# The shared expert's parts moved among the encoder's last two sequences, with VectorE norms in closer slots for these and a gate computed on GpSimd

## The chip, the cores and the metric

The kernel runs on one core of a Trainium2 chip. The metric is the device time of one execution in microseconds (us). Engines are named as in the profile: PE is TensorE, PEld its weight loads, DVE is VectorE, ACT is ScalarE, POOL is GpSimd, SP is SyncE, which issues most of the DMAs.

## The reference, cut to what matters

Eight sequences of 256 tokens with 128 features pass through four blocks with residual additions. The change touches the end of the first (six encoder layers) and the second (a mixture of experts); the third is a state-space block, the fourth two layers of local attention.

```python
x = x + encoder(layernorm(x))              # 6 layers, 16 heads
x = x + experts(layernorm(x))              # 8 experts, top 1, and a shared one
x = x + state_space(layernorm(x))
x = x + local_attention_layers(layernorm(x))

# one encoder layer
w_avg = softmax(q k^T / sqrt(8)).mean(over heads)
sa = softmax(w_avg + rel) @ h
h1 = LN(h + sa, l1);  h2 = LN(h1, l2)
ff = relu(h2 @ w1.T + b1) @ w2.T + b2
h  = LN(h2 + ff, l3)

# experts, per token
score = x @ router; e = argmax(score); gate = sigmoid(score[e])
routed = silu(gate*x @ w1[e]) * (gate*x @ w3[e]) @ w2[e]
shared = silu(x @ ws1) * (x @ ws3) @ ws2
out = routed + shared
```

Everything is fp32; F is 352 in the experts and 512 in the encoder.

## The kernel before, in words

**Order of work.** Within each of the stages the order of all instructions is written out by hand. `at(slot, order, fn)` puts a step into a table; the steps are then issued by slot, within a slot by `order`, and within that in order of insertion (routes first, then shared parts and blocks, then the encoder's plans). Each engine has a queue that takes its instructions in this order and waits at the first whose data aren't there. A slot is thus a place in the order and no time.

**Encoder.** `plan(n, l, b)` lays out layer l of sequence b, with n = 8l + b from 0 to 47 and t0 = 16n: the attention scores and their exponentials fill the slots t0-12 to t0+19, the rest of the layer follows in the `r_` steps, from the transpose of the mixing weights (t0+21) by mix (t0+29), norm 1 (t0+32), norm 2 (t0+36), transpose (t0+38), the feed-forward network (two halves `r_ff1` at t0+40 and t0+44, `r_ff2` at t0+47) to norm 3 (t0+58). So two to three sequences overlap. `r_norm1`, `r_norm2`, `r_residual` and `r_norm3` run on POOL, by the helpers `normal_pool` (L247, L249) and `affine` (L102, L103); mean and variance (`mean_var`, L235, L237) run on DVE, and 1/sqrt as an addition and a power on POOL (`rsqrt`, L81, L82). In the last layer norm 3 also adds the sequence into x (L481). The softmax weights need `dg` (L332) from POOL and the row sums' inverse `z` (L330) from DVE.

**Routing.** `route(b, t0)` follows each sequence of the last layer from its slot t0+59 on, one step a slot: statistics, 1/sqrt, norm (POOL), transpose (PE, L556), copy (ACT, L560), scores (PE, L565), `choose` (six DVE operations from L573 to L582; L577 is one of them; and exp(-top) on ACT, L584), `count` (PE, L594 to L598), `gate` (DVE, L588, L589: 1/(1 + exp(-top))), `put` (DVE: positions in the bucket, to L612), and `send` (POOL: scaling by the gate, L617, and two scatter DMAs, L619, into the bucket in HBM).

**Experts.** Behind the last route `table` (DVE, from L633 to L657) counts the blocks of each expert, and PE and SP load the results into registers. `shared(q, t0)` is the shared expert for sequences 2q and 2q+1: three times two matmuls (`up`, L750), Silu on ACT (L757), product on DVE (L761), `down` (PE, L767), copy (ACT, L771), transposes (PE, L776), two additions into x (DVE, L781). Parts 0 and 1 stand between table and blocks, parts 2 and 3 behind the blocks. `block(j, t0)` is one of 23 blocks of 128 routed tokens: load from the bucket (SP, L687), transpose (PE, L692), up, Silu, product, transpose, down, copy (DVE, L734) and store to `routed` (SP, L735).

**After the experts.** The state-space stage begins with a gather of `routed` (POOL, four indirect DMAs for two sequences, L887), the additions (DVE, L894), a norm, a transpose, a convolution (PE) and Silu (ACT, L978). Behind the experts SP issues the loads of the last stage's weights (L1148), whose tiles lie where the experts' weights were.

**PSUM.** `bank()` takes the next of six banks, which the attention scores use also; `small_bank()` one of two, which everything else of the encoder uses.

Of the kernel before, what the change touches and what calls it, by code (L numbers as in the profile page):

```python
# [10 lines left out]
F32 = mybir.dt.float32  # L11
# [7 lines left out]
P = 128  # L19
# [36 lines left out]
def model_kernel(ctx: ExitStack, tc: tile.TileContext, A: dict, out: bass.AP):  # L56
# [42 lines left out]
    def affine(dst, src, w, b):  # L99

        shape = [P, src.shape[1], P]
        nc.gpsimd.tensor_tensor(dst, src, w.unsqueeze(1).to_broadcast(shape), ALU.mult)  # L102
        nc.gpsimd.tensor_tensor(dst, dst, b.unsqueeze(1).to_broadcast(shape), ALU.add)  # L103
# [77 lines left out]
    with ExitStack() as s0:  # L181
# [63 lines left out]
        def normal_pool(dst, src, mv, rs):  # L245
            neg = small.tile([P, NC], F32, name="neg", tag="neg", bufs=2)
            nc.gpsimd.tensor_scalar(neg, mv[:, :, 0], -1.0, None, ALU.mult)  # L247
            for i in range(NC):
                nc.gpsimd.tensor_scalar(  # L249
                    dst[:, i, :], src[:, i, :], neg[:, i : i + 1], rs[:, i : i + 1], ALU.add, ALU.mult  # L250
                )

        def plan(n, l, b):
            t0 = SLOTS * n
            v = {}

# [155 lines left out]
            def r_norm1():  # L412
                ln = v["w"][2]
                normal_pool(v["t1"], v["t1"], v["mv1"], v["rs1"])
                affine(v["t1"], v["t1"], ln[:, 0, :], ln[:, 1, :])

            def r_norm2():
                n2 = wk.tile([P, NC, P], F32, name="n2", tag="n2")
                normal_pool(n2, v["t1"], v["mv2"], v["rs2"])
                v["n2"] = n2  # L420

            def r_residual():
# [3 lines left out]
                affine(v["h2"], v["n2"], ln[:, 2, :], ln[:, 3, :])  # L426
# [47 lines left out]
            def r_norm3():  # L474
                ln = v["w"][2]
                hn = hp.tile([P, NC, P], F32, name="h", tag=f"h{b}")
                normal_pool(hn, v["t2"], v["mv3"], v["rs3"])
                affine(hn, hn, ln[:, 4, :], ln[:, 5, :])
                hs[b] = hn
                if l == DEPTH0 - 1:  # L480
                    nc.gpsimd.tensor_tensor(xs[b], xs[b], hn, ALU.add)  # L481
# [6 lines left out]
            at(t0 + 29, 4, r_mix)  # L488
            at(t0 + 30, 5, r_add)
            at(t0 + 31, 5, lambda: put("rs1", lambda: inv_std(v["mv1"], 1)))  # L490
            at(t0 + 32, 6, r_norm1)
            at(t0 + 35, 5, lambda: put("mv2", lambda: mean_var(v["t1"], 2)))
            at(t0 + 36, 5, lambda: put("rs2", lambda: inv_std(v["mv2"], 2)))
            at(t0 + 36, 6, r_norm2)
            at(t0 + 37, 6, r_residual)
            at(t0 + 38, 4, r_transpose2)
            at(t0 + 39, 5, r_h2t)
            at(t0 + 40, 4, lambda: r_ff1(0))
            at(t0 + 41, 5, lambda: r_relu(0))
            at(t0 + 44, 4, lambda: r_ff1(1))  # L500
            at(t0 + 45, 5, lambda: r_relu(1))
            at(t0 + 47, 4, r_ff2)
            at(t0 + 48, 5, r_add3)
# [1122 lines left out]
```

## Time and profile before

| what | us |
|---|---|
| median of 3 runs | 2029.11 (2028.04 to 2031.71) |
| profiled execution, its own time | 2033.83 |
| its span, first to last instruction | 2032.1 |
| busy in the span: PE, DVE, ACT, POOL | 1715.8, 1430.8, 1283.9, 1116.2 |
| norm 3 with x of sequence 7 (the last) ends | 1091.8 |
| last route's positions, table | 1101.6, 1104.6 |
| shared parts 0 and 1 on PE | 1107.0 to 1126.6 |
| blocks, to the last copy | 1126.6 to 1181.2 |
| shared parts 2 and 3, to the last addition | 1181.2 to 1198.9 |
| first addition of gathered rows begins | 1207.1 |

The table's places in time are us from the span's start. The page of the profile gives busy times, then the span in 40 slices (each digit the busy share in tenths, PEclk the granted TensorE clock), DMA queues, and the costliest groups of instructions. An engine that is busy three quarters of the span may set the time in one stage and idle in the next, so the stages are read one by one.

### The profile page before, as it was taken

The numbers are of one execution on the slowest core, as the hardware profiler recorded it, in microseconds if no ns is written. First come the engines' busy times: TensorE is split into PE (matmuls) and PEld (weight loads), VectorE is DVE, ScalarE is ACT, GpSimd is POOL, SyncE is SP. The second block draws the span as 40 slices with busy tenths as digits, with TensorE's granted clock in tenths as the row PEclk, the third lists the DMA queues.
The fourth block names the chain that finished last, engine by engine and source line by source line (L and its number), as shares of the span: only waits on it lengthen the run. The fifth ranks groups of instructions, "written<-read, shape, count | busy, mean of one in ns | idle before, by whom it ended". The sixth has DMA issues, their size and how long they took to land. (4 is left out here: it accounts for less than half of the span.)

```text
span 2032.1 us, 38679 instructions
## 1 busy us (share of the span) xinstructions
PE 1715.8 (84%) x13390; PEld 1009.4 (50%) x13406; DVE 1430.8 (70%) x3308; ACT 1283.9 (63%) x4576; POOL 1116.2 (55%) x1663
## 2 busy tenths in 40 slices
PE   5899999999999999997864968687676898888987
PEld 2565656565656566555542733122222655555554
DVE  4787787787878787876632435988897677666664
ACT  4887888888888888886520324544522666666654
POOL 2576777777777777776773024767464333233221
PEclk9999999999999999999975989888877899999989
DMA  9200000000000000000000120000000000000000
GB/s 305 66 2 1 24 2 2 14 11 2 15 10 2 9 17 2 2 1 6 4 8 12 41 93 4 5 6 1 0 0 1 1 1 1 1 1 1 6 6 11
DMA packets 43218, 35.52 MB, mean 17 GB/s; under 512 B 3957, under 2 KB 39055, under 8 KB 43023
## 3 DMA queue, kind: packets, MB, share of 16 engines
q1 hardware_dynamic: 41423, 30.63, 4.9%
q8 instruction: 108, 1.77, 0.4%
q0 software_dynamic: 1024, 2.10, 0.3%
q14 instruction: 87, 0.71, 0.1%
q10 hardware_dynamic: 576, 0.31, 0.1%
HBM read 20.57 MB, written 12.45 MB: 16 GB/s over the span
## 5 line engine op out<-in xcount | busy, mean ns | idle before, releaser
L322 ACT ACTIVATE e<-s,nmax 128x256 f32<-128x256 f32 x1536 | 709.1, 492 | 81.7 <-DVE nmax L318 77.9
L318 DVE TENSOR_REDUCE nmax<-s 128x2 f32<-128x512 f32 x768 | 493.6, 670 | 151.8 <-PE s L308 151.8
L322 ACT ACTIVATION_READ_ACCUMULATOR e<-s,nmax 128x1 f32 x1536 | 343.8, 224 | 0.0
L308 PE MATMUL s<-kt,qm 32*128 32x256 f32 x3072 | 305.1, 422 | 17.1 <-ACT e L322 14.5
L359 PE MATMUL pacc<-e,dg 128*32 128x256 f32 x3072 | 257.2, 396 | 41.3 <-POOL dg L332 27.9
L308 PEld LDWEIGHTS s<-kt,qm 32*128 32x128 f32 x3072 | 184.2, 189 | 114.9 <-ACT e L322 64.8
L1076 POOL TENSOR_TENSOR hc<-h,bc 128x1024 f32<-128x1024 f32 x64 | 155.5, 2434 | 116.1 <-DVE h L1069 109.7
L1298 POOL TENSOR_TENSOR r<-r,r 128x512 f32<-128x512 f32 x64 | 81.1, 1271 | 231.3 <-DVE r L1279 195.1
L332 POOL TENSOR_TENSOR dg<-sel,z 128x256 f32<-128x256 f32 x192 | 118.5, 617 | 133.8 <-DVE z L330 114.7
L1058 ACT ACTIVATE da<-pd,na 128x510 f32<-128x510 f32 x128 | 80.8, 682 | 167.8 <-PE pd L1041 156.1
L359 PEld LDWEIGHTS pacc<-e,dg 128*32 128x32 f32 x3072 | 95.6, 110 | 164.8 <-POOL dg L332 60.4
L1069 DVE TENSOR_TENSOR_SCAN h<-da,pu 128x1024 f32<-128x1024 f32 x64 | 146.3, 2287 | 8.5 <-ACT da L1058 0.5
L81 POOL TENSOR_SCALAR rs<-mv 128x2 f32<-128x2 f32 (+1 forms) x192 | 44.1, 230 | 191.5 <-DVE mv L237 96.5
L82 POOL TENSOR_TENSOR rs<-rs,mhalf 128x2 f32<-128x2 f32 (+1 forms) x192 | 139.4, 726 | 15.7
L1041 PE MATMUL pu<-u,ssel 32*128 32x512 f32 x256 | 97.5, 768 | 49.9 <-DVE h L1069 40.0
L1355 ACT ACTIVATE el<-sl,nm,rn 128x128 f32<-128x128 f32 x256 | 114.0, 466 | 39.5 <-DVE nm L1346 39.3
L1255 PE MATMUL pq<-wqkv,y 128*128 128x512 f32 x224 | 121.4, 629 | 1.0 <-issue 1.0
L369 ACT ACTIVATE nw<-pacc 128x256 f32<-128x256 f32 x96 | 36.9, 384 | 116.8 <-PE pacc L355 115.9
L447 PE MATMUL pf<-h2t,wa 128*128 128x256 f32 x384 | 106.9, 402 | 2.4 <-DVE h2t L436 2.4
L463 PE MATMUL po<-wf,r 128*128 128x128 f32 x768 | 104.9, 294 | 0.0
L463 PEld LDWEIGHTS po<-wf,r 128*128 128x128 f32 x768 | 96.9, 205 | 13.6 <-DVE st L235 13.6
L1067 DVE TENSOR_TENSOR pu<-pu,bc 128x1024 f32<-128x1024 f32 x64 | 77.8, 1215 | 19.9 <-PE pd L1041 19.8
(271 smaller groups left out, 3507.7 us busy)
## 6 DMA issues: line engine op xcount, KB each, us to landing
bucket<-zrow SPq DMA_DIRECT2D x1, 8640.0 KB, 29.5
ln<-in_ln_dram SPq DMA_DIRECT2D x6, 448.0 KB, 3.7
wa<-in_wa_dram SPq DMA_DIRECT2D x6, 384.0 KB, 3.1
wf<-in_wf_dram SPq DMA_DIRECT2D x6, 256.0 KB, 6.3
wqkv<-in_wqkv_dram SPq DMA_DIRECT2D x1, 1536.0 KB
xb<-bucket SPq DMA_DIRECT2D x23, 64.0 KB, 1.8
routed<-ob SPq DMA_DIRECT2D x23, 64.0 KB, 1.5
w<-in_w1e_dram SPq DMA_DIRECT2D x1, 1408.0 KB, 32.0
```

The source lines that it names most:

```text
L82: nc.gpsimd.tensor_tensor(dst, dst, mhalf.to_broadcast(list(dst.shape)), ALU.pow)
L308: nc.tensor.matmul(ss[g][:, i, :], v["qm"][rows, 2 * k + i].rearrange("p j q -> p (j q)"), v["kt"][rows, :], start=True, stop=True,)
L318: nc.vector.tensor_reduce(v["nmax", k][:, g, :], v["s", k][g], AX.X, ALU.max, negate=True)
L322: nc.scalar.activation(v["e", k][:, g, i, :], v["s", k][g][:, i, :], AF.Exp, bias=v["nmax", k][:, g, i : i + 1], accum_out=v["z", k][:, g, ...
L332: nc.gpsimd.tensor_tensor(dg, sel32.unsqueeze(1).to_broadcast(sh), z.unsqueeze(2).to_broadcast(sh), ALU.mult)
L359: nc.tensor.matmul(acc, v["dg", k][:, 2 * g + i, :], v["e", k][:, g, i, :], start=(g == 0), stop=False,)
L447: nc.tensor.matmul(pf[:, i, :], v["w"][0][:, f0 : f0 + P], v["h2t"], start=True, stop=True)
L463: nc.tensor.matmul(po[:, c, :], v["r"][:, f, c * P : (c + 1) * P], v["w"][1][:, f, :], start=(f == 0), stop=(f == 3),)
L1069: nc.vector.tensor_tensor_scan(h.rearrange("p h t -> p (h t)"), da, pu.rearrange("p h t -> p (h t)"), 0.0, ALU.mult, ALU.add)
L1076: nc.gpsimd.tensor_tensor(hc, v["h", n], v["bc", 1].unsqueeze(1).to_broadcast([P, 2, T2]), ALU.mult)
L1255: nc.tensor.matmul(pq, yb[:, col : col + P], wqkv[:, l, i * INNER : (i + 1) * INNER], start=True, stop=True)
L1355: nc.scalar.activation(v["e", c][:, par, j, :], v["s", c][par][:, j, :], AF.Exp, scale=v["rn", c][:, 0, h : h + 1], bias=v["nm", c][:, par ...
```

## The change

- **Closer slots.** For n of 46 and 47 (`tail`) the steps behind the attention stand closer: mix at t0+23 (was 29), norm 1 at t0+26, transpose at t0+30 (38), the second half of the network four slots behind the first's base (was six), norm 3 at t0+40 (58). Norm 3 of sequence 5 in the last layer stands at t0+50. Each route of the last layer follows its norm 3 by a slot.
- **Engines.** Norms 1, 2 and 3 of these two with their affines (not the residual's) and the last addition into x run on DVE; so do the norm and the scaling of `send` in routes 6 and 7. The 1/sqrt and the scatters stay on POOL. Routes 4 to 7 take their PSUM from the six banks.
- **Gate.** exp(-top) leaves ACT: POOL multiplies by -1 and raises e to that power, in the slot of `choose`, behind it.
- **Shared expert.** Part 0 begins at slot 776 (t0 of the last sequence, 752, and 24), part 1 at 790, part 2 at 798; the table stands at 804, part 3 at 805, the blocks from 814. `up` comes last in its slot now (order 8, was 4), and the parts use six-bank PSUM throughout. Nothing but a load of ACT's exponential table stands behind the blocks.

```diff
-        def normal_pool(dst, src, mv, rs):
+        def normal(eng, dst, src, mv, rs):
+            if eng is nc.vector:
+                for i in range(NC):
+                    eng.tensor_scalar(
+                        dst[:, i, :], src[:, i, :], mv[:, i, 0:1], rs[:, i : i + 1], ALU.subtract, ALU.mult
+                    )
+                return
...
+        last3 = [58] * (NB - 3) + [50, 40, 40]
...
+            tail = n >= DEPTH0 * NB - 2
+            eng = nc.vector if tail else nc.gpsimd
...
-                normal_pool(v["t1"], v["t1"], v["mv1"], v["rs1"])
-                affine(v["t1"], v["t1"], ln[:, 0, :], ln[:, 1, :])
+                normal(eng, v["t1"], v["t1"], v["mv1"], v["rs1"])
+                affine(eng, v["t1"], v["t1"], ln[:, 0, :], ln[:, 1, :])
...
-            at(t0 + 29, 4, r_mix)
...
-            at(t0 + 58, 6, r_norm3)
+            t1, t2, t3 = (t0 + 23, t0 + 30, t0 + 40) if tail else (t0 + 29, t0 + 38, t0 + 58)
+            if l == DEPTH0 - 1:
+                t3 = t0 + last3[b]
+            at(t1, 4, r_mix)
...
+            t2 = t2 + (4 if tail else 6)
...
+            at(t3, 6, r_norm3)
...
+        euler = c0.tile([P, 1], F32, name="euler", tag="euler")
+        nc.vector.memset(euler, np.e)
...
+            eng = nc.vector if b >= NB - 2 else nc.gpsimd
+
+            route_bank = bank if b >= NB - 4 else small_bank
...
-                nc.scalar.activation(top, top, AF.Exp, scale=-1.0)
                 v["top"] = top
+
+            def decay():
+
+                nc.gpsimd.tensor_scalar(v["top"], v["top"], -1.0, None, ALU.mult)
+                nc.gpsimd.tensor_tensor(v["top"], euler.to_broadcast([P, NC]), v["top"], ALU.pow)
...
-                at(t0 + k, 4, lambda k=k: up(k))
+                at(t0 + k, 8, lambda k=k: up(k))
...
-        first_free = SLOTS * (DEPTH0 * NB - 1) + 59
+        def exp_table():
+            nc.scalar.preload_act_table_set("natural_log_exp_and_others")
+
         for b in range(NB):
-            route(b, SLOTS * ((DEPTH0 - 1) * NB + b) + 59)
-        e0 = first_free + 11
+            route(b, SLOTS * ((DEPTH0 - 1) * NB + b) + last3[b] + 1)
+        end = SLOTS * (DEPTH0 * NB - 1)
+
+        shared(0, end + 24)
+        shared(1, end + 38)
+        shared(2, end + 46)
+        e0 = end + last3[-1] + 12
         at(e0, 1, table)
-        shared(0, e0 + 1)
-        shared(1, e0 + 4)
-        e1 = e0 + 12
+        shared(3, e0 + 1)
+        e1 = e0 + 10
         for j in range(MB):
             block(j, e1 + j)
         at(e1 + 4, 9, where)
-        e2 = e1 + MB + 3
-        shared(2, e2)
-        shared(3, e2 + 3)
+        at(e1 + MB + 4, 9, exp_table)
```

## The prediction

> **What bounds the kernel now.** I read the slices of the page first, to find the stages, then the chain, then stretches of 10 us, then each engine's queue in order of time. Columns of a queue row: start and length in us, engine, line, operation, out<-in; in brackets the idle time before it and what ended it.
>
> ```profile
> span 2032.1 us, 38679 instructions
> ...
> PE   5899999999999999997864968687676898888987
> ...
> POOL 2576777777777777776773024767464333233221
> PEclk9999999999999999999975989888877899999989
> ```
>
> A slice is 50.8 us. Slices 20 to 23 (1016 to 1219 us) hold the end of the encoder, the routing, the experts and the gather; PE drops and its clock falls to half. The chain of waits does not reach so far back (its longest pieces begin at 1569 us), so here the queues must speak.
>
> ```profile
> 1050.00:1060.00 10.00, 6.93 (x32) 6.61 (x32) 4.02 (x24) 0.58 (x2) 6.91 (x16) 0.50 0.01 2
> ...
> 1080.00:1090.00 10.00, 1.83 (x10) 1.76 (x10) 1.35 (x9) 0.06 (x1) 4.83 (x9) 0.55 0.03 13
> ...
> 1150.00:1160.00 10.00, 10.00 (x63) 7.85 (x62) 4.12 (x13) 4.45 (x13) 0.00 (x0) 1.00 0.21 59
> ```
>
> Busy us of PE, PEld, DVE, ACT, POOL, then PE's clock. From 1040 to 1107 nobody is full: one sequence's chain passes from engine to engine, a latency bound. The 23 expert blocks (1150 row) are bound by PE. The stages' ends, from the queues:
>
> ```profile
> 1101.40 0.17 DVE L612 CAST pos<-place 128x2 int32<-128x2 f32 x1
> ...
> 1104.38 0.19 DVE L657 CAST tabi<-tab 128x46 int32<-128x46 f32 x1
> ...
> 1106.95 7.76 PE L750 MATMUL pe<-xnt,w 128*128 128x512 f32 x12 [6.28 <-issue]
> ...
> 1126.62 0.27 PE L692 MATMUL pk<-ident,xb 128*128 128x128 f32 x1
> ...
> 1180.87 0.29 DVE L734 COPY ob<-pk 128x128 f32<-128x128 f32 x1 [0.49 <-PE pk L727]
> ...
> 1193.87 0.40 SPq L1148 DMA_DIRECT2D wqkv<-in_wqkv_dram x1
> ...
> 1198.86 0.98 POOL L887 DMA_INDIRECT yg<-routed,pickup  x1 [92.42 <-DVE x L781]
> ...
> 1207.11 0.43 DVE L894 TENSOR_TENSOR x<-x,yg 128x256 f32<-128x256 f32 x1 [8.26 <-DMA rot<-in_rot_dram]
> ```
>
> Last route's positions known 1101.6; table 1104.6; shared parts 0 and 1 on PE 1107.0 to 1126.6; blocks from there to 1181.2; shared parts 2 and 3 until 1198.9, and only then the gather, whose first addition runs at 1207.1 (the second at 1208.2).
>
> **Part 1: shared parts 2 and 3 leave the end.** Nothing stands then between the last block and the gather. The last routed store follows the copy at 1181.2 and lands 1.5 us later (median of that DMA), so the four gathers are issued from about 1183 to 1188 (0.95 us each, 0.3 between). What is late next: the weights of the last stage. They are loaded as soon as the expert weights are free, today 1193.9, and keep the DMA engines full until about 1207; they now start behind the last store, at 1181.6, 12.8 us of traffic, to 1194.4. Bounds for the second addition: 2.4 us after the issue (unloaded landing, the row's minimum) is 1190.3; 6.5 us (its maximum, under these same loads) 1194.4. Before it was 1208.2: gain 13.8 to 17.9. I take 14.5, near the loaded end, since the loads are the same ones.
>
> **Part 2: the table of ScalarE.** The Silu table is now loaded during the encoder; sequence 7's Relus run under it. The page "ScalarE: Activation LUTs" of the Trainium skill (Table sets) says that relu is in every set, and (What ACT_TABLE_LOAD costs) that a switch costs 1.28 us plus a drain, 2.66 in all. The trace shows 1.28 and Silu and Copy mixed without a load; Relu among them no run shows.
>
> ```profile
> 1097.94 1.28 ACT L757 ACT_TABLE_LOAD   x1
> ...
> 1222.22 0.69 ACT L978 ACTIVATE xc<-pm,colm 128x512 f32<-128x512 f32 x1 [24.87 <-PE pm L955]
> ```
>
> The new preload behind the blocks and the Silu load that it forces before L978 are two loads, 2.6 us by the row and 5.3 by the page; ACT idles 24.9 us there, so nothing. Without that cover they would cost that sum.
>
> **Part 3: the gate's power.** It leaves ACT (0.20 us, eight times) for POOL: a product and a power on 128x2, priced by L81 and L82 at 0.23 + 0.72, with gaps 1.1 us. Cover, for routes 0 to 3 in full encoder work, is POOL's idle time behind the power of norm 3:
>
> ```profile
> 979.08 0.71 POOL L82 TENSOR_TENSOR rs<-rs,mhalf 128x2 f32<-128x2 f32 x1
> ...
> 980.44 0.16 DVE L588 TENSOR_SCALAR top<-top 128x2 f32<-128x2 f32 x1
> ...
> 982.22 0.66 POOL L332 TENSOR_TENSOR dg<-sel,z 128x256 f32<-128x256 f32 x1 [2.43 <-PE pacc L355]
> ```
>
> It would end at 980.9, but DVE wants it at 980.4 for the gate, and queued behind the gate are the statistics, nmax and z, for which POOL's dg waits. So 0.55 us on the path; the same at route 3, none at routes 0 and 1 (951.4 against 951.9). Sum +1.1. A gain from ACT's freed wait (2.3 us at that exp) I put at nothing, as DVE runs there without idle time. Ends: 0 and 1.1 x 4.
>
> **Part 4: the tail, walked along the queues** with the rows' durations, in the clock of the trace before. Slots give each queue's order.
> - x of sequence 5: 1048.5 before, now 1044.9. Its norm 3 on POOL comes earlier, but sequence 6's statistics and Relu wait on DVE behind route 4's and 5's statistics, which wait for POOL.
> - Route 4's send holds POOL for 4.1 us (two scatters, 1.1 + 2.0 + 1.0) until 1052.0, then route 5's norm until 1053.3. PE's transpose of route 5 waits for it, and behind it stand sequence 7's mix and part 0's matmuls. So r_add of sequence 7 runs at 1055.4 (before 1049.9).
> - x of sequence 6, now on DVE: 1059.0 (before 1071.3), a gain of 12.
> - Part 0 takes PE at 1056 and brings Silu and product into ACT's and DVE's queues. Three pairs of matmuls at 1.9 to 2.6, three products at 0.69, three downs at 0.9, copy 0.6, transposes 0.6, additions 0.75: sequence 7's norm 1 ends at 1064.1, its second mean and the gate of route 5 wait behind the third product (1066.6), its transpose runs behind part 0's (1072.6).
> - Route 6's power is behind route 5's send and a residual on POOL (1076.5), and DVE's gate and second Relu behind it (1078.7). ff2 ends 1081.4, the addition 1082.7, part 1's first two products stand before norm 3: x of sequence 7 at 1089.0 (before 1091.8).
> - Route 7: part 1's and then all of part 2's products stand in its DVE queue: statistics 1091.1, norm 1092.9, scores 1095.0, choice 1099.5 (behind part 2's first product), gate 1105.3 (behind the third), positions 1106.3. Before: 1101.6.
> - Table 3.1, PE's register loads 2.4 (1104.6 to 1107.0), part 2's transposes 0.6, part 3 alone 11.7 (7.5 cold matmuls, then Silu, product, down, copy, transposes): first block at 1124.1. The scatters (issued by 1111.1, 2.3 to land) and block loads (1.8) are done by then.
> - Scatters start 0.8 after positions, not at once as I let sends 4 and 5 do: +1.2. With part 3's +1.1, 1126.4.
>
> Before: 1126.6. The closer slots and the part less ahead of the blocks are paid back by the waits that the parts bring: about 5 for part 0, 5 for part 1, 7.5 for part 2. The end that I am unsure of is 17 us earlier (no wait counts) to 10 later.
>
> **A rule against it.** The Trainium skill, "SBUF — State Buffer", Who interferes with whom: a VectorE operation with two SBUF inputs and a GpSimd one that reads SBUF exclude each other, for the whole instruction. The trace agrees:
>
> ```profile
> 977.95 0.73 POOL L103 TENSOR_TENSOR t<-t,ln 128x256 f32<-128x256 f32 x1
> ...
> 978.08 0.62 DVE L577 TENSOR_TENSOR choice<-sc,top 128x16 f32<-128x16 f32 x1
> ```
>
> 0.62 where it takes 0.17 alone: it ends with POOL's. The change moves ten such operations (affines and residuals of two sequences) to DVE. By the rule at its worst, 10 x 0.73 = 7.3 us; by the queues POOL computes only beside sequence 6's norm 1, +1.1, which the walk holds. I take 1.1.
>
> **Sum.** Blocks start -0.2, rounded to +0.5 as their first row has a second wait at 1127.7; blocks unchanged at 54.5; gather -14.5. Together -14.0: the profiled execution, 2033.83 us (span 2032.1 and 1.7 around it), becomes 2019.8. The median of the runs is 2029.11, 4.7 below the profiled one, so 2015.1.
>
> **Rivals.**
> - The parts really lie in gaps: the waits of Part 4 (17.5) don't stand in the path. Blocks start near 1110, total -30: 1999. For it: PE and ACT are idle most of 1040 to 1107. Against: queues are in order and DVE is needed by both.
> - The tail runs longer than walked by 8 to 10 (cold PE, port waits at 7.3): -4 to -6, 2024.
> - Slower: one mechanism, the power with a running exponent costs more than L82's constant one. Each of eight routes waits for it on DVE; at 2.9 us or more in place of 0.72 the loss is 8 x 2.2 = 17.5, which eats the 14 and 0.2%: 2034 at 3 us. Against: L82 grows 0.72 to 1.04 from two to four elements, a per-element price that shows no sign of a special case.
> - The gather gains nothing because the weights' loads merely move ahead of it: excluded beyond 1194.4 by their 12.8 us.
>
> **Numbers.** Forecast's own case 0.63 (2008 to 2021), free parts 0.13, longer tail 0.17, slow power 0.05, others 0.02. A measurement here tells 0.2%, 4 us. Range 2003 to 2025 leaves out the far half of the first rival and the slow power. Faster 0.88: own case, free parts and most of the longer tail. Same 0.06, slower 0.06.
>
> **What would show it.** Right: no shared matmuls behind the last block, the first gather about 2 us behind the last store, positions of route 7 near 1109, one part (12 us) between table and first block. Wrong: positions before 1100 (free parts) or beyond 1118; a power row far above 0.72; a table load beside a Relu; the first addition more than 14 us behind the last copy.

## The result, and the profile after

The median fell from 2030.41 us (2028.04 to 2036.32) to 2003.30 us (2002.59 to 2003.60), a ratio of 0.9862 with a 95% interval of 0.9840 to 0.9884. The forecast was 2015.1: direction right, gain 27.1 us in place of 14.0. The time lies at the lower edge of the range (2003 to 2025), and the gain exceeds the 26.1 us that this edge stood for (2029.11 less 2003). The profiled execution took 2002.59 us (span 2000.8), 0.7 below its median; that of before, 2033.83, lies 3.4 above its own.

The slices of the changed kernel's page, here one slice is 50.0 us:

```profile
span 2000.8 us, 38671 instructions
...
PE   5899999999999999998768867687666898888987
...
POOL 2477777777777777777763024767564332233221
PEclk9999999999999999998888979888878999999999
DMA  9200000000000000000000310000000000000000
```

Slices 20 and 21, at a clock of 0.7 and 0.5 before, now show 0.8, and the second burst of DMA traffic, the late weights (the loads of the last stage's weights), has moved one slice earlier, into the one that holds the first half of the blocks. Stretches of 10 us of the changed kernel (busy us of PE, PEld, DVE, ACT, POOL, then PE's clock):

```profile
1050.00:1060.00 10.00, 7.93 (x22) 4.79 (x22) 3.73 (x13) 2.85 (x4) 3.99 (x8) 0.66 0.03 8
1080.00:1090.00 10.00, 9.03 (x26) 3.69 (x24) 6.66 (x21) 2.61 (x5) 3.12 (x6) 1.00 0.04 13
...
1150.00:1160.00 10.00, 10.00 (x60) 7.80 (x59) 4.41 (x14) 4.22 (x13) 0.00 (x0) 1.00 0.19 54
```

Where PE was 1.83 us busy at a clock of 0.55 (1080 to 1090), it is now 9.03 busy at 1.00. The stages' ends, from the changed kernel's queues:

```profile
1100.22 0.17 DVE L636 CAST pos<-place 128x2 int32<-128x2 f32 x1
...
1103.49 0.19 DVE L681 CAST tabi<-tab 128x46 int32<-128x46 f32 x1
...
1106.08 1.09 PE L800 MATMUL pe<-ident,e 128*128 128x128 f32 x4 [5.55 <-issue]
1106.96 4.65 PE L774 MATMUL pe<-xnt,w 128*128 128x512 f32 x8
...
1117.33 0.38 PE L716 MATMUL pk<-ident,xb 128*128 128x128 f32 x2
...
1127.95 0.40 SPq L1176 DMA_DIRECT2D wqkv<-in_wqkv_dram  x1
...
1134.75 0.30 PE L716 MATMUL pk<-ident,xb 128*128 128x128 f32 x1 [1.59 <-DMA xb<-bucket]
...
1174.50 0.29 DVE L758 COPY ob<-pk 128x128 f32<-128x128 f32 x1 [0.49 <-PE pk L751]
...
1177.37 1.00 POOL L915 DMA_INDIRECT yg<-routed,pickup  x1 [49.03 <-issue]
...
1181.73 0.43 DVE L922 TENSOR_TENSOR x<-x,yg 128x256 f32<-128x256 f32 x1 [6.94 <-DMA yg<-routed,pickup]
1183.75 0.42 DVE L922 TENSOR_TENSOR x<-x,yg 128x256 f32<-128x256 f32 x1 [1.60 <-DMA yg<-routed,pickup]
```

| end of the stage | before | after | moved | forecast |
|---|---|---|---|---|
| positions of route 3 (start of the cast) | 1011.43 | 1011.24 | -0.2 | +1.1 |
| positions of route 7 | 1101.40 | 1100.22 | -1.2 | about +5, extras included +7 |
| first block's transpose | 1126.62 | 1117.33 | -9.3 | -0.2 |
| last block's copy ends | 1181.16 | 1174.79 | -6.4 | -0.2 |
| second addition of the gather | 1208.17 | 1183.75 | -24.4 | -14.0 |
| first scan of the state space | 1250.67 | 1227.33 | -23.3 | |
| end of the span | 2032.1 | 2000.8 | -31.3 | -14.0 |

So 9.3 us come ahead of the blocks, where nothing was forecast; the blocks give 2.9 back (54.5 to 57.5 us), because the late weights are loaded beside them and PE waits for `xb` (the 1.59 above); and the stretch from last copy to second addition falls from 27.0 to 9.0 us, 18.1 in place of 14.5. A sentence on the kernel before is wrong here: the late weights' tiles do not lie where the experts' weights were. Their loads start at 1127.95, while the blocks still read those; before, SP's queue waited 12.2 us for the last `up` of shared part 3 on PE (L750), which reads `xnt`. Of the median's 27.1 us the marks up to the second addition hold 24.4; what lies behind them is taken up in the last section.

### The profile page after: what moved, and what is told of

Same layout as the page of the kernel before. It is cut to its first block, busy times and chain, and to the rows that moved or that the text cites. A ratio compares the mean times of both kernels' runs of the same rounds, so it can differ in the third digit from the quotient of the medians.

```text
span 2000.8 us, 38671 instructions
## 1 busy us (share of the span) xinstructions
PE 1702.5 (85%) x13390; PEld 999.1 (50%) x13406; DVE 1441.5 (72%) x3339; ACT 1285.3 (64%) x4570; POOL 1107.4 (55%) x1641
## 5 line engine op out<-in xcount | busy, mean ns | idle before, releaser
L371 PE MATMUL pacc<-e,dg 128*32 128x256 f32 x3072 | 257.5, 396 | 41.7 <-POOL dg L344 28.5
L82 POOL TENSOR_TENSOR rs<-rs,mhalf 128x2 f32<-128x2 f32 (+1 forms) x192 | 140.4, 732 | 15.7
L475 PEld LDWEIGHTS po<-wf,r 128*128 128x128 f32 x768 | 93.6, 198 | 16.9 <-DVE st L235 13.6
L302 POOL TENSOR_TENSOR qm<-qt,kmask 128x1024 f32<-128x1024 f32 x48 | 90.9, 1895 | 0.4 <-DVE qt L291 0.4
```

The lines of the kernel that those rows point to most:

```text
L82: nc.gpsimd.tensor_tensor(dst, dst, mhalf.to_broadcast(list(dst.shape)), ALU.pow)
L371: nc.tensor.matmul(acc, v["dg", k][:, 2 * g + i, :], v["e", k][:, g, i, :], start=(g == 0), stop=False,)
L475: nc.tensor.matmul(po[:, c, :], v["r"][:, f, c * P : (c + 1) * P], v["w"][1][:, f, :], start=(f == 0), stop=(f == 3),)
```

## Experiments

A mark is the start of an instruction in one profile. Marks are counted below from the cast to positions of route 3, since up to there the kernels do nearly the same work and their profiles are shifted by up to 5 us against each other. The theory, **T1**, is the prediction's walk: the parts bring in-order waits into the tail that pay back most of what the closer slots gain. Its rival **R1**: the gaps are nearly free, and the closer slots bring little.

| kernel | route 7's positions | first block | blocks, us | last copy to second addition | first scan | median us | ratio to before |
|---|---|---|---|---|---|---|---|
| before | 89.97 | 115.19 | 54.5 | 27.0 | 239.2 | | |
| changed kernel | 88.98 | 106.09 | 57.5 | 9.0 | 216.1 | 2003.30 | 0.9862 (0.9840 to 0.9884) |
| noparts | 77.96 | 95.00 | 56.9 | 9.0 | 202.7 | 1990.73 | 0.9814 (0.9789 to 0.9839) |
| tailonly | 77.95 | 103.13 | 54.5 | 27.7 | 227.1 | 2023.94 | 0.9983 (0.9973 to 0.9993) |
| partsonly | 110.66 | 127.96 | 56.7 | 9.3 | 235.5 | 2024.58 | 0.9991 (0.9977 to 1.0004) |
| part2late | 84.16 | 109.87 | 56.5 | 9.0 | 217.3 | 2005.09 | |
| powonly | 93.54 | 118.78 | 54.6 | 27.7 | 243.0 | 2033.71 | 1.0034 (1.0021 to 1.0046) |
| slotspool | 85.78 | 102.49 | 56.9 | 9.0 | 210.3 | 1998.14 | |
| loadslate | 88.96 | 106.25 | 54.6 | 12.5 | 216.4 | 2002.17 | 0.9888 (0.9859 to 0.9916) |
| nopreload | 88.92 | 106.36 | 57.5 | 8.9 | 214.0 | 1998.29 | |
| gateact | 86.30 | 103.81 | 57.3 | 9.0 | 211.5 | 2000.07 | |
| gateact_timed | 86.41 | 103.91 | 56.9 | 9.0 | 211.4 | 2003.38 | 0.9894 (0.9877 to 0.9911) |
| fill1 | 79.08 | 95.87 | 57.1 | 9.0 | 203.6 | 1990.61 | |
| fill2 | 78.68 | 96.87 | 57.4 | 9.0 | 205.6 | 1994.95 | |
| fillbefore | 91.30 | 117.09 | 54.5 | 27.1 | 241.6 | 2031.44 | 1.0007 (0.9998 to 1.0016) |
| after_again | 89.45 | 106.83 | 57.0 | 9.0 | 214.2 | 2000.79 | 0.9864 (0.9848 to 0.9880) |
| after_beside | 89.40 | 106.74 | 57.3 | 8.9 | 214.3 | 2002.92 | 0.9875 (0.9857 to 0.9893) |
| part3behind | 89.41 | 99.78 | 56.7 | about 10 | 210.2 | 1995.57 | 0.9848 (0.9832 to 0.9864) |
| part3_again | 86.57 | 97.00 | 56.4 | about 10 | 207.0 | 1999.75 | 0.9863 (0.9845 to 0.9880) |
| both | 88.99 | 99.53 | 56.7 | about 10 | 209.6 | 2000.53 | 0.9872 (0.9855 to 0.9888) |

A median without a ratio is one single time. The kernel before had medians of 2026.2 to 2029.2 us beside these runs; noparts, slotspool, fill1 and fill2 leave out the shared expert's share for sequences 0 to 5.

How well marks come back is seen where one kernel has several profiles. The changed kernel (after_again and after_beside are the same) agrees with itself to 0.5 us at route 7's positions and to 1.9 at the first scan. But part3behind and part3_again, which are one kernel too, are 2.8 us apart at route 7's positions and at the first block, and 3.2 at the first scan. So a difference below about 3 us between two single profiles is not safe at these marks.

### The parts and the closer slots, each alone

**noparts**

```diff
-        shared(0, end + 24)
-        shared(1, end + 38)
-        shared(2, end + 46)
```

> The changed kernel without parts 0, 1 and 2 of the shared expert (it leaves out the shared expert's share for sequences 0 to 5; all else stands). Theory T1, the prediction's walk: the three parts bring about 17.5 us of in-order waits into the tail of the encoder, which pays the gain of the closer slots back, so without them the positions end near 1083 instead of 1100.4, the first block's transpose stands near 1100 instead of 1117.3, and the time is about 1986. Rival R1: the gaps are nearly free, the parts cost under 6 us together, and the closer slots bring little of their own: positions at 1094 or later, first block at 1111 or later, time 1997 or more.

The positions stand at 1088.2, 11.0 us earlier than with the parts when both are counted from route 3; the first block is 11.1 earlier, the time 12.6 lower. R1 is refuted, since the gaps are not free; T1 holds in kind, but its 17.5 us were 11.0 (11.0 to 11.5 over the changed kernel's three profiles; tailonly, without the parts in the tail too, stands within 0.01 us of noparts).

The waits themselves are in the changed kernel's trace. VectorE's waits at rows of the parts in the tail (tile, line, what it waited for, us, times, longest), and the gate of route 7 behind part 2's third product:

```profile
DVE e L785 <- PE pe L774: 9.2, 5, 3.5
...
DVE x L805 <- PE pe L800: 1.5, 2, 1.3
DVE e L785 <- ACT e L781: 1.4, 1, 1.4
```

```profile
1098.67 0.68 DVE L785 TENSOR_TENSOR e<-e,pe 96x512 f32<-96x512 f32 x1 [3.52 <-PE pe L774]
1099.27 0.16 DVE L612 TENSOR_SCALAR top<-top 128x2 f32<-128x2 f32 x1
```

VectorE's queue stood 12.1 us at products and additions of the parts, 10.7 of them until PE had done a matmul of the part.

**tailonly** (the parts at their old places)

```diff
-        shared(0, end + 24)
-        shared(1, end + 38)
-        shared(2, end + 46)
...
-        shared(3, e0 + 1)
-        e1 = e0 + 10
+        shared(0, e0 + 1)
+        shared(1, e0 + 4)
+        e1 = e0 + 12
...
+        shared(2, e1 + MB + 3)
+        shared(3, e1 + MB + 6)
```

> The closer slots, VectorE's norms and the power stay; the shared parts go back to their old places (0 and 1 between table and blocks, 2 and 3 behind the blocks). T1 (closer slots alone bring some 17 to 19 us at the positions): positions near 1083, then 3.3 to the table's end and the 22 us that two parts took before, first block near 1109, the stretch from last copy to second addition again near 27 us with the late loads in it; time about 2030.4 - 18 = 2012. R1 (closer slots bring under 6 us): positions 1095 to 1101, first block 1120 or later, time 2024 to 2030.

The closer slots with VectorE's norms bring 12.0 us at the positions and 12.1 at the first block (15.6 at the positions against powonly below, which has the power's cost in it as tailonly has), and the 27.7 us behind the blocks return. The expectation's 17 to 19 had been worked out loosely: the recorded walk, without its 17.5 of waits, has 1088.8 against 1101.6, thus 12.8, and that is right. The time falls by only 2.7 us (0.9983), at the edge of R1's range and far from T1's 2012, and by less than the marks; the last section comes back to this.

**partsonly** (the parts moved, with the old slots and GpSimd's norms)

```diff
-        last3 = [58] * (NB - 3) + [50, 40, 40]
+        last3 = [58] * NB
...
-            tail = n >= DEPTH0 * NB - 2
+            tail = False
...
-            eng = nc.vector if b >= NB - 2 else nc.gpsimd
+            eng = nc.gpsimd
...
-        shared(0, end + 24)
-        shared(1, end + 38)
-        shared(2, end + 46)
+        shared(0, end + 30)
+        shared(1, end + 48)
+        shared(2, end + 64)
```

> Parts 0 to 2 stand in the tail and part 3 between table and blocks, but the tail has its old slots and GpSimd's norms (the power stays). T1: the parts cost 5 to 17.5 us there: positions at 1107 to 1119, first block at 1124 to 1136, then the 15 us of the stretches behind it (-18.0 behind the blocks, +2.9 in them): time 2010 to 2022. R1: the old tail's gaps hide the parts as well as the new one's: positions near 1101 to 1103, first block 1118 to 1120, time 2003 to 2006, no slower than the whole change.

The positions stand at 1121.9, later than even T1 had them. Against powonly, which has the same slots of the tail and the same power, the parts cost 17.1 us in the old tail (110.66 less 93.54); in the changed tail they cost 11.0. So the closer slots with VectorE's norms are also what makes the parts cheap, though the parts' own places differ between the two as well (slots 30, 48, 64 against 24, 38, 46). In time neither half is worth more than 0.2%, the whole 1.4%.

**part2late** (part 2 between table and blocks)

```diff
-        shared(2, end + 46)
-        shared(3, e0 + 1)
-        e1 = e0 + 10
+        shared(2, e0 + 1)
+        shared(3, e0 + 4)
+        e1 = e0 + 12
```

> The changed kernel with part 2 moved out of route 7's chain to between table and blocks, ahead of part 3. T1 (part 2 costs 7.5 us in the chain, as the walk had it): positions near 1093, then 3.3 and 22 us: first block 1117 to 1119, time as the whole change's, 2003 to 2005. R1 (part 2 costs under 2 us in the chain): positions 1098.5 to 1100.5, first block 1124 to 1126, time 2009 to 2012.

Part 2 costs 4.8 us in route 7's chain (walked: 7.5; without it 1095.4, nearer T1's 1093 than R1's), which leaves 6.2 for parts 0 and 1 (walked: 10). The positions of routes 5 and 6 split these. Part 1 is issued behind both, so only part 0 can delay them, and with the parts they stand 56.7 and 65.5 us behind route 3's, in noparts 51.7 and 60.5. So part 0 costs 5.0, just as walked, and part 1 the remaining 1.2 (walked: 5), if part 0's delay reaches route 7 whole. Between table and blocks part 2 costs 8.6 us (22.25 with two parts, 13.65 with one). The gain ahead of the blocks is then the sum of three terms: closer slots -12.0, three parts in the tail +11.0, one part fewer between table and blocks -8.4 (22.05 before, 13.65 after); together -9.4, against 9.1 counted from route 3.

**slotspool** (noparts with GpSimd's norms)

```diff
-            eng = nc.vector if tail else nc.gpsimd
+            eng = nc.gpsimd
...
-            eng = nc.vector if b >= NB - 2 else nc.gpsimd
+            eng = nc.gpsimd
```

> The closer slots without parts 0 to 2 (the shared expert's share for sequences 0 to 5 is left out) and with GpSimd's norms as before: it splits the 15.6 us between the power alone (positions of route 7 at 93.54 behind those of route 3) and the closer slots with VectorE's norms (77.96). Theory V: VectorE's norms bring most of it, since VectorE waited 26.8 us for GpSimd's additions in that tail: 86 to 92. Theory S: the slots bring most of it, the engine under 4 us: 78 to 82.

The positions stand at 85.8. From 93.5 to 78.0 the slots bring one half (7.8 us) and VectorE's norms the other (7.8), each from single profiles; neither theory had equal halves. The slots' half includes the PSUM banks of routes 4 to 7, which no run changed alone; nor does one change the place of `up` within its slot alone.

### The late loads

**loadslate**

```diff
...
                 nc.vector.tensor_copy(ob, v["po"][:, 0:P])
+                if j == MB - 1:
+                    nc.vector.tensor_copy(touch, ob[:, 0:1])
...
+        at(-30, 0, lambda: nc.vector.tensor_copy(wqkv[:, 0, 0:1], touch))
         for k, (t, src) in enumerate(late_loads):
             at(4 + k, 9, lambda t=t, src=src: nc.sync.dma_start(t, src))
```

> The changed kernel, but the late weights' loads wait for the last block's copy, so they run beside the first gather instead of during the blocks. T1 (loads and gather are one term of fixed size that only moves): blocks from first transpose to last copy 54.5 to 55 us instead of 57.5, the second addition 15 to 22 us behind the last copy instead of 9.0, time 4 to 10 us above the changed kernel. R1 (the loads cost nothing where they stand; the stretch of 27 us before came from the shared parts alone): the second addition stays at 9 to 11 us behind the last copy and the time within 2 us of the changed kernel, or 3 us below it by the faster blocks.

The queues of loadslate, last copy, first of the late loads and the additions:

```profile
1171.75 0.29 DVE L759 COPY ob<-pk 128x128 f32<-128x128 f32 x1 [0.49 <-PE pk L752]
...
1172.58 0.40 SPq L1180 DMA_DIRECT2D wqkv<-in_wqkv_dram  x1
...
1182.21 0.43 DVE L925 TENSOR_TENSOR x<-x,yg 128x256 f32<-128x256 f32 x1 [9.79 <-DMA yg<-routed,pickup]
1184.54 0.43 DVE L925 TENSOR_TENSOR x<-x,yg 128x256 f32<-128x256 f32 x1 [1.90 <-DMA yg<-routed,pickup]
```

The blocks are as fast as before (54.6), and the gather, now beside the loads, takes 12.5 us in place of 9.0: 2.9 won, 3.5 lost, first scan and time unchanged. T1 was right that the loads only move and too high in their price (it had 15 to 22 us, and 4 to 10 us more time); the time is as R1 had it. If the terms simply add, the 27.0 us of before were about 14.5 for the shared parts 2 and 3 (27.0 less 12.5), 3.5 for the loads and 9.0 for the gather.

### The gate's power and ScalarE's tables

**powonly** (the kernel before with `decay` in place of L584)

```diff
+        euler = c0.tile([P, 1], F32, name="euler", tag="euler")
+        nc.vector.memset(euler, np.e)
...
-                nc.scalar.activation(top, top, AF.Exp, scale=-1.0)
...
+            def decay():
+                nc.gpsimd.tensor_scalar(v["top"], v["top"], -1.0, None, ALU.mult)
+                nc.gpsimd.tensor_tensor(v["top"], euler.to_broadcast([P, NC]), v["top"], ALU.pow)
...
```

> The kernel before with the gate's power on GpSimd alone. Prediction's term: +0.55 at each of routes 2 and 3, +1.1 us at the first block. Rival by the trace after (route 3's send stood at 1014.72 against 1014.83): within 0.3 us of before at the positions of routes 3 and 7. Rival that the removed table loads pay: up to 2.6 us earlier. Time within the measurement of before for all three; the marks tell them apart.

Slower by 0.34%, with route 7's positions 3.6 us later; no expectation had that. Of the 3.6 us, 2.5 are there at route 4 and another 1.5 come between routes 5 and 6. VectorE's queue of route 5 in powonly, and the waits of VectorE over the whole tail (engine, tile, line, what it waited for, us, times, longest):

```profile
1061.33 0.17 DVE L584 TENSOR_TENSOR choice<-first,moec 128x16 f32<-128x16 f32 x1
1062.68 0.17 DVE L592 TENSOR_SCALAR top<-top 128x2 f32<-128x2 f32 x1 [1.17 <-POOL top L589]
```

```profile
DVE top L592 <- POOL top L589: 5.1, 4, 2.2
```

The same place before:

```profile
1057.73 0.17 DVE L582 TENSOR_TENSOR choice<-first,moec 128x16 f32<-128x16 f32 x1
1057.82 0.16 DVE L588 TENSOR_SCALAR top<-top 128x2 f32<-128x2 f32 x1
```

The exponential on ScalarE (L584, from 1057.38 for 0.20 us) was done by the time VectorE wanted it; in powonly the product and power on POOL were not:

```profile
1060.82 0.71 POOL L82 TENSOR_TENSOR rs<-rs,mhalf 128x2 f32<-128x2 f32 x1
1061.62 0.23 POOL L588 TENSOR_SCALAR top<-top 128x2 f32<-128x2 f32 x1
1061.93 0.71 POOL L589 TENSOR_TENSOR top<-euler,top 128x2 f32<-128x2 f32 x1
```

The row itself has L82's price, 0.71 us, so the rival of a slow power is refuted; it costs by standing behind another power on the same queue, in the last four routes, where the chain is the bound. The forecast term of 0.55 us at route 2 is real too, though marks counted from route 3 hide it: from route 1's positions to route 2's it is 28.5 us in each of the five profiles without the power, and 29.1 to 29.6 in the fifteen with it. At route 3 the profiles do not settle it (28.8 to 29.6 from route 2 without, 29.1 to 30.1 with).

**gateact**, and **gateact_timed**, the same kernel again

```diff
+                nc.scalar.activation(top, top, AF.Exp, scale=-1.0)
...
-                (6, 6, decay), (7, 4, count), (8, 5, gate), (9, 5, put), (10, 6, send),
+                (7, 4, count), (8, 5, gate), (9, 5, put), (10, 6, send),
```

> The changed kernel with the gate's exponential back on ScalarE, the closer slots and the parts as they are. ScalarE then has to change tables between Silu and exponential in the tail: at 1.28 us a load, 4 to 6 loads. Theory: each that lies in the chain of parts or route adds its 1.28 us, positions 2 to 6 us later (1102 to 1106) and first block with them, time 2005 to 2010. Rival: ScalarE's gaps hide all loads, positions within 0.5 us of 1100.2, so the power only saves GpSimd's 1 us and the time is the same or lower.

> The changed kernel with the exponential on ScalarE again, now timed. Theory (the power costs more than the table loads that it saves): positions of route 7 at 86.3 behind route 3's, where the changed kernel has 88.98, and a time 2 to 4 us under its 2003.3. Rival (the gain is taken back by TensorE's clock): the same marks, and a time within 1 us of 2003.3.

Neither had the direction of the first run: the positions come 2.6 us earlier, in both profiles. The timed median is the changed kernel's own, 2003.38 against 2003.30, as the second run's rival said. ScalarE does change tables in between; its queue in gateact:

```profile
1056.99 1.28 ACT L604 ACT_TABLE_LOAD   x1 [1.30 <-DVE choice L598]
1058.28 0.20 ACT L604 ACTIVATE top<-top 128x2 f32<-128x2 f32 x1
1058.50 1.28 ACT L782 ACT_TABLE_LOAD   x1
1059.80 0.60 ACT L782 ACTIVATE e<-pe 128x512 f32<-128x512 f32 x1
```

Each change costs 1.28 us and 0.02 around it. The page "ScalarE: Activation LUTs" of the Trainium skill (What ACT_TABLE_LOAD costs) puts 2.66 on a change with its drain; by that, an estimate for the three loads that begin from 1056.99 to 1068.49 is 8.0 us; by the rows they are 3.8, and the rows decide. That the power costs in the changed kernel is shown as far as route 6: there the gate waited 3.50 us for POOL (at 1075.78), in gateact 0.53 for ScalarE, and route 6's positions stand at 65.5 in the three profiles of the changed kernel, at 62.0 and 62.1 in those of gateact. At route 7 it isn't shown: the 2.6 us are within what two profiles of one kernel differ by, and in the profile of both, with the same exponential, the positions stand at 88.99, where part3behind without it gave 89.4 once and 86.6 once.

**nopreload**

```diff
-        at(e1 + MB + 4, 9, exp_table)
```

> The changed kernel without the exponential's table load behind the last block, so Silu's table stays in and the load in front of the first Silu of the state space goes. If that load stands on the path as read (1.28 us beside 23.74 of idle time that the matmul ended): first Silu 1.28 us earlier (near 1198.7), first scan 0 to 1.3 us earlier. If TensorE paces the stretch, as the later marks say: first scan within 0.3 us, though the Silu is earlier.

The changed kernel's ScalarE around the preload that this run drops:

```profile
1173.65 1.28 ACT L817 ACT_TABLE_LOAD   x1
1198.68 1.28 ACT L1006 ACT_TABLE_LOAD   x1 [23.74 <-PE pm L983]
1199.97 0.69 ACT L1006 ACTIVATE xc<-pm,colm 128x512 f32<-128x512 f32 x1
```

Silu's load doesn't run in the 23.74 idle us ahead of it: it waits with the activation that needs it, and then stands in front of it. Dropping it moved the first scan by 2.1 us against the first profile of the changed kernel, but by 0.3 and 0.4 against the two later ones (214.2 and 214.3), although the first Silu comes 1.6 us earlier behind the last copy than in those two. That is the second expectation; what the load costs on the path is too little to tell from nothing.

### The clock

The walk was made in the clock of the trace before. Between the positions of routes 3 and 7 that was 0.67; in the changed kernel it is 0.85, without the parts 0.72. Two runs put TensorE work that nobody reads in the parts' place, a third does so in the kernel before:

```diff
+        def filler():
+            for i in range(1):            # fill2: range(2)
+                t = bank()
+                nc.tensor.matmul(t[:, 0 : 2 * P], w1[:, NE, 0:P], xnts[0][:, 0 : 2 * P], start=True, stop=True)
+        for k in range(24, 52):           # fillbefore: range(24, 70)
+            at(end + k, 8, filler)
```

> The kernel without parts 0 to 2 (the shared expert's share for sequences 0 to 5 is left out), with 28 matmuls of 128x256 whose result nobody reads, one in each slot from the start of part 0 to the end of part 2: TensorE work alone, about 13 us at full clock, with no ScalarE or VectorE row behind it. Theory C (the parts also raise the granted clock of the tail, from 0.72 without them to 0.85 with them, and this is why the walk in the old clock ran 6 us late): granted clock between the positions of routes 3 and 7 at 0.78 or more, and route 7's positions at 77 or less behind route 3's in spite of the added work (77.96 without it). Theory O (the walk was late by overlapping rows, the clock has no part): the added matmuls only delay, positions at 79 to 84.

> As the run with 28 unread matmuls, with 56 of them, two a slot: about the 26 us of TensorE that parts 0 to 2 have. C: granted clock 0.85 or more, positions at 76 to 80, as the higher clock and the added work cancel; the 11 us that the parts cost are then their ScalarE and VectorE rows. O: positions at 83 to 90, the parts' cost is TensorE's time.

> The kernel before with 46 unread matmuls of 128x256, one a slot through the tail and the last route, and nothing else changed. C: granted clock in the tail 0.75 or more instead of 0.67, positions of route 7 at 86 to 89 instead of 89.97, time 1 to 4 us under the kernel before. O: positions at 91 or later, time not lower.

The clock rises as theory C said (0.80, 0.84, and 0.79 in fillbefore); the chain isn't shortened as it said: 79.1, 78.7 and 91.3 against 78.0 and 90.0. Route 7 on PE in noparts:

```profile
1081.61 0.73 PE L577 MATMUL pe<-ident,xn 128*128 128x128 f32 x2 [8.52 <-DVE xn L248]
1082.80 1.02 PE L586 MATMUL pe<-router,xnt 128*128 128x8 f32 x4 [0.46 <-ACT xnt L581]
...
1086.87 0.57 PE L622 MATMUL pe<-choice,ones 128*128 128x8 f32 x2
```

```profile
1076.22:1088.18 11.96, 4.06 (x16) 3.50 (x16) 5.16 (x23) 1.66 (x2) 2.85 (x6) 0.54 0.02 6
```

and in fill2:

```profile
1082.56 0.49 PE L577 MATMUL pe<-ident,xn 128*128 128x128 f32 x2 [0.68 <-DVE xn L248]
1082.88 1.89 PE L826 MATMUL pe<-xnt,w 128*128 128x256 f32 x8
1084.61 0.51 PE L586 MATMUL pe<-router,xnt 128*128 128x8 f32 x4
...
1087.60 0.37 PE L622 MATMUL pe<-choice,ones 128*128 128x8 f32 x2
```

```profile
1076.02:1088.70 12.68, 12.00 (x64) 10.44 (x63) 6.14 (x29) 1.66 (x2) 3.75 (x7) 1.00 0.02 7
```

The chain's own rows shrink (1.02 to 0.51, 0.57 to 0.37), and yet the positions come no earlier: here the transpose's matmuls are followed by queued fillers. Two things follow. Matmuls that no other engine waits for cost next to nothing in the tail: between the positions of routes 3 and 7 PE is 45.4 us busy in noparts, 63.2 in fill2 and 68.7 in the changed kernel, and fill2's positions are only 0.7 us later. So most of the 11.0 us come through the parts' Silus and products and the rows that stand behind them. It does not follow that the parts' matmuls are free: VectorE's products waited for them (the 9.2 us under noparts), and they come in bursts, which the evenly spread fillers do not copy. And rows from a cold stretch are too long for a warm one.

**after_again** is the changed kernel once more.

> The changed kernel itself, in the same call as the others and with the kernel before on the same chip: by the runs so far 2003 against 2026 to 2030. It shows whether its marks and its granted clock (0.85 in the tail; positions 88.98, first scan 216.1 behind route 3's positions) come back in another profile, which says how much of a difference of 2 us between two kernels' marks is the clock's: theory C has the marks up to the first block within 0.3 us, and the stretch behind the first scan free to differ by some us; the rival has both the same.

The marks up to route 6 came back within 0.04 us, route 7's positions to 0.5, the first block to 0.7, the first scan to 1.9, at the same mean clock in the tail (0.85). Theory C had 0.3 up to the first block. With part3behind and part3_again below, 2.8 us apart at the first block, even this is not the widest spread.

### A version with part 3 behind the blocks

**part3behind**, **part3_again** (the first gather is issued ahead of part 3 and lands in the tile of `xnts[0]`; beside it, the changed kernel as after_beside), and **both** (that with gateact's edit, without the preload)

```diff
-        shared(3, e0 + 1)
-        e1 = e0 + 10
+        e1 = e0 + 4
...
+        at(e1 + MB + 3, 0, collect_first)
+        shared(3, e1 + MB + 3)
+        at(e1 + MB + 10, 9, pick_first)
```

> The changed kernel with part 3 behind the blocks, beside the first gather, which is issued ahead of it into a tile that is free by then. Theory: 8.4 us less between table and first block (13.65 to about 5.2), the blocks 54.7 us since the late loads wait for part 3, second addition 11 to 13 us behind the last copy instead of 9: first scan 7 to 9 us earlier, time 1994 to 1997. Rival: the late loads now collide with the gather and part 3 stands ahead of the state space on TensorE anyway, second addition 18 us or more behind the last copy: time 2000 to 2004.

> Part 3 behind the blocks and the exponential on ScalarE, without its table's load behind the blocks. Theory: the gains add up, positions 2.7 us earlier, first scan 10 to 13 us earlier than in the changed kernel, time 1990 to 1994. Rival: one of the two gains is lost, time 1995 to 2000.

> Part 3 behind the blocks once more, now beside the changed kernel on the same chip. By the marks (first block 6.3 to 7.1 us earlier behind route 3's positions, last copy 7.1 to 7.3, first scan 4.1 to 5.9): median 4 to 8 us under the changed kernel's, ratio to before near 0.984. Rival (TensorE's clock behind the blocks takes it back, as it did for the exponential on ScalarE): the two within 2 us.

> The changed kernel beside it: median 2000 to 2003, ratio to before 0.986 to 0.987, and marks as in its two profiles so far (positions 89.0 to 89.5, first block 106.1 to 106.8, last copy 163.6 to 163.8, first scan 214 to 216 behind route 3's positions).

The queue of VectorE in part3_again, from the last copy over part 3's additions to those of the gather:

```profile
1163.35 0.29 DVE L758 COPY ob<-pk 128x128 f32<-128x128 f32 x1 [0.49 <-PE pk L751]
...
1172.66 0.75 DVE L805 TENSOR_TENSOR x<-x,pe 128x256 f32<-128x256 f32 x2 [2.55 <-PE pe L800]
1173.33 0.75 DVE L830 TENSOR_TENSOR x<-x,xnt 128x256 f32<-128x256 f32 x2
```

Part 3 fits into the time of the gather: 6.7 to 6.9 us less between table and first block, and from last copy to first scan 53.6 to 53.7 us where the changed kernel has 50.3 to 52.5. On one chip the first scan is 7.3 us earlier than the changed kernel's and the last scan 7.4. But 2.8 of these stand already at route 7's positions, which part 3 does not touch and which part3behind has at 89.41; from there to the first scan it is 4.5 us (120.4 against 124.9). The median is 3.2 lower (1999.75 against 2002.92), short of the 4 to 8 expected: four times each, 1997.60 to 2000.95 against 2002.10 to 2003.21, but after_again had 1999.23 to 2003.42. On another chip the ratio of part3behind was 0.9848. The version beats the kernel before by 1.4 to 1.5%; that it beats the changed kernel in time is likely and not settled. The exponential on ScalarE on top (both) added nothing: 2000.53, above what either of its expectations had.

## Why the prediction was wrong

- **Part 4, the step that failed.** Its sum of the waits, "about 5 for part 0, 5 for part 1, 7.5 for part 2", was too large: 11.0 in place of 17.5. Part 0 cost 5.0 as walked; the terms of parts 1 and 2 in route 7's chain were mis-sized, 1.2 and 4.8 in place of 5 and 7.5 (each from one profile of part2late). The mechanism held (VectorE's queue stood 12.1 us at the parts' rows), and so did the closer slots' share (12.8 walked, 12.0 measured). The walk meets the trace at the end of sequence 7's second Relu (1078.7 in both), in part by luck, since x of sequence 6 came 1.2 us earlier than walked and the addition of mix in sequence 7 started 0.7 earlier. From there to the positions it ran 5.9 us late. There (1078 to 1101) the clock was 0.57 in the trace that the durations came from and 0.99 in the new one: transposes 0.91 to 0.40, scores 1.02 to 0.61, five counts 0.43 to 0.22 apart, ff2 3.29 to 2.56, together 2.7 us. The other 3.2 are put down to whole durations added where rows in fact overlap; no run separates the two.
- **Extras.** The +1.2 for the scatters didn't appear, and the stretch from positions to first block was 16.9 in place of 17.8. With Part 3's +1.1, which the marks counted from the span's start do not have, this makes the 9.1 us between forecast and first block.
- **Part 3.** The +1.1 was put on routes 2 and 3. At route 2 the 0.55 is there (0.6; the rows shown, 980.89 against 980.44, give only 0.45), at route 3 it stays open; the -0.2 of the first table can't tell, as profiles are shifted against each other by more. What the term put at nothing were the last four routes, 3.6 us in the old slots. In the changed kernel Part 4 did walk the power at route 6, and rightly (done at 1076.5 walked, 1075.7 in the trace).
- **Part 1.** Loads beside the gather were forecast at up to 13.2 us from copy to second addition; loadslate measured 12.5. What failed is where the loads stand: Part 1 let them start behind the last store, but nothing holds them once VectorE's last read of the routing's tiles (L703) is done. So they started at 1127.95 and ran beside the blocks, 2.9 us dearer there and 3.5 us saved behind them. The bounds of 13.8 to 17.9 left this out; the measured 18.1 is just beyond. For blocks and gather together 14.5 was forecast and 15.2 measured, which is luck: both terms were off.
- **Part 2.** Relu ran under Silu's table without a load, as said. The forced load wasn't hidden, but cost nothing that the marks can show. The load of Silu's table in the tail had no price: it stands at 1057.33, behind part 0's first matmuls and not ahead of them, and VectorE's first product waited 1.4 us for the Silu behind it.
- **The rule of the port.** VectorE's affines beside POOL took 0.57 where they take 0.43 alone, 0.3 us in all; neither 7.3 nor the 1.1 taken. In these rows neither engine waited the other's instruction out (POOL's 0.89 took 1.03).
- **The sum.** At the second addition -24.4: ahead of the blocks -9.3, blocks +2.9, gather -18.1 (rounded). What the forecast's sum called rounding, -0.2 to +0.5 at the blocks' start, added 0.7 us; without it the sum is -14.7. The median's other 2.7 us lie behind this mark, and their cause stays open. The total came near the first rival's size (-30) by another way: its cause, free gaps, is refuted by noparts.

## What to carry to other kernels

Price a moved piece of work in each place where it can stand: a shared part cost 8.6 us between two stages, 1 to 5 in a latency chain that leaves the engines idle, and one to three beside a gather, so the gain was the difference of two prices and not either of them. Work that fills TensorE's gaps also changes its clock, so durations from a cold stretch are upper bounds for a warm one. When the last reader of a tile moves, look for the transfers that were waiting for it: they will start earlier, beside something else.

## What the runs showed of the hardware

- TensorE's granted clock rose with its load: 0.54 with 4.06 of 11.96 us busy, 1.00 with 12.00 of 12.68 in the same place, though still 0.50 with 6.93 of 10 in the kernel before (1050 to 1060). The page "TensorE: Matmul & The Clock Gate" of the Trainium skill (What's actually happening) says that the clock is half by default and that activity releases it, which these rows show. Read as advice to keep the engine warm it would promise the 0.2 to 0.5 us that each of the chain's rows became shorter; measured, the positions with unread matmuls in the tail are 0.7 to 1.3 us later, and in no run earlier.
- Behind the last scan all these kernels have the same work, and yet the stretch from there to the end took from 483.3 (part2late) to 492.7 us (tailonly) in the profiles, 490.6 before and 484.5 after, with dips of the granted clock at different places (the 15 us behind the last scan: 0.62 before, 0.69 after). The profile of before is itself a long execution, 2033.83 us, 3.4 to 7.6 above the medians of that kernel; fillbefore, the same work there, took 485.1. So marks and medians need not agree: 12 us at the first scan were 2.7 in tailonly's median, 7.3 were 3.2 in part3_again's, and 23 were 27 in the changed kernel's. What sets the pattern was not found.
